# Layer 0 preparation: offset range by ScalarE sums of Relu, and a third depthwise tap on TensorE

## The chip, the cores and the metric

The kernel runs on one core of a Trainium2 chip. The metric is the device time of one execution in microseconds, as the median of several runs; lower is better. A NeuronCore has five engines with instruction queues of their own: TensorE (PE in the profile, with its weight loads as PEld), VectorE (DVE), ScalarE (ACT), GpSimd (POOL) and SyncE (SP). Each works off its queue in order and waits on semaphores for the others. DMA transfers are issued from the queues of SyncE, ScalarE or GpSimd.

## The reference

A four layer network on an input of 8 images of 56 x 56 pixels with 128 channels. Only the first half of layer 0, a deformable convolution, is touched:

```python
xp = x @ w_in + b_in
h = conv3x3_depthwise(x, dw_w) + dw_b
h = (h - bn_m) * bn_g / sqrt(bn_v + 1e-05) + bn_b
h = gelu(h)
offset = (h @ w_off + b_off).reshape(N, H, W, 4, 9, 2)
mask = softmax((h @ w_msk + b_msk).reshape(N, H, W, 4, 9), axis=-1)
y = dcn_core(xp, offset, mask) @ w_out + b_out
...
```

`dcn_core` samples `xp` bilinearly at nine points per pixel and group, each shifted by its own offset, and sums them with the mask. The rest of layer 0 is a norm, an MLP and a second norm. Layer 1 is a whitening transform of the whole tensor, layer 2 attention with a mixture of experts, layer 3 linear attention with another. They are not touched.

## The kernel before

`conv_layer` prepares, for all 8 images, what the sampling needs, and keeps it in device memory: the input transposed (`q.xT`), offsets and mask (`q.om`), and the projection `xp` in overlapping strips with a border of zeros (`q.strips`). Then one number decides on the branch: if no offset is larger than 1 in size, `sample_near` runs, otherwise `sample_any` in a loop over the images. The branch is at L400 and L401. With these inputs `sample_near` is taken, and its first instruction on GpSimd, the memset of `wide` (L467), waits for the last transfer of `om`.

The preparation is one loop over n from -1 to 8 with functions that are called in this order: `hidden` of image n-1, `image` and `first_taps` of image n+1, `other_taps` of image n, after every odd image `projection` of the pair, and `offsets` of image n-1. Images lie in pairs in two tiles `xp0` and `xp1`, with borders of zeros.

- `image` (L257): one load of `xs` by SyncE; 28 transposes on TensorE into PSUM (`p_x`, L266); seven copies to the padded image by ScalarE (L271); seven shifted copies `xT` by ScalarE (L276), each written to device memory by SyncE (L279). `xT` has two buffers.
- `first_taps` (L309): the first `NTE` of the nine taps of the depthwise convolution as matmuls with diagonal matrices (`taps`, made at L223), in seven groups of eight image rows, accumulated in PSUM (`p_dw`, L315) and copied to `acc` by ScalarE (L322). `NTE` is 2.
- `other_taps` (L325): the taps left over, seven per image, on VectorE: `acc = xp * dw + acc` over 128 x 3136 elements (L327).
- `hidden` (L336): seven Gelus on ScalarE with the folded batch norm (L341), to `hT`.
- `offsets` (L350): 28 matmuls (`p_om`, L356), seven adds of the bias on VectorE (L363), the largest and the smallest offset by two reductions on VectorE (L365, L366), the mask's softmax (`mask_softmax`, L424 to L435: maximum, subtraction, Exp on ScalarE at L432, sum, reciprocal, product, the others on VectorE), and the write of `om` by SyncE (L370).
- `projection` (L281): 56 matmuls per pair (`p_in`, L288), 14 adds of the bias on VectorE (L295), and twelve writes to `strips` by SyncE (L301 to L305).

All these share one PSUM pool of eight buffers (tag "m"), so a matmul group starts only when a buffer has been read out. Tiles of the pool `l0h` (`xs`, `xT`, `acc`, `hT`, `om`, `pj`, `msum`) have two buffers. The order of the instructions in each queue is not that of the text: a scheduler interleaves the functions of different images by its own estimate of durations. After the loop, L393 takes the largest entry of `far` per partition, a transpose (L395) and L397 the largest of all, and L398 compares it with 1.

Before the loop GpSimd clears the tile `zero` (L237), and ScalarE's queue issues its transfers into the borders of `strips`: two large ones (L240) and sixteen small ones (L245). Its first copy L271 comes behind these.

Of the kernel before, what the change touches and what calls it, by code (L numbers as in the profile page):

```python
# [8 lines left out]
F32 = mybir.dt.float32  # L9
I32 = mybir.dt.int32  # L10
U32 = mybir.dt.uint32
AF = mybir.ActivationFunctionType
ALU = mybir.AluOpType
AX = mybir.AxisListType
# [3 lines left out]
NB, IH, IW, C = 8, 56, 56, 128  # L18
S = IH * IW
T = 112  # L20
NT = S // T
# [6 lines left out]
GP = GRP * NP  # L28
# [3 lines left out]
VW = IW + 4  # L32
PH, PX, NX = 7, 4, 14
SW = PX + 4
# [1 line left out]
R4 = 4 * C  # L36

NPX = 6
NTE = 2


WB, WCOLS, WSTEP, WITER, WEPS = 64, NB * S * C // 64, 9, 5, 0.01
# [85 lines left out]
def conv_layer(tc, k, x, w, z):  # L128

    nc = tc.nc  # L130
    n_batch = x.shape[0]
    with ExitStack() as ctx:
        cp = ctx.enter_context(tc.tile_pool(name="l0c", bufs=1))
# [62 lines left out]
        gam = row_bc(nc, cp, w["gamma2"], T, "gam2r")  # L196
        nc.vector.tensor_tensor(q.sft2, q.sft2, gam, ALU.mult)

        far = cp.tile([T, 2 * n_batch], F32, name="far")
        near = cp.tile([1, 1], I32, name="near")  # L200
        with ExitStack() as pre:
            ip = pre.enter_context(tc.tile_pool(name="l0i", bufs=1))
# [11 lines left out]
                "b_om",  # L214
            )
            b_om = b_om.unsqueeze(1).to_broadcast([T, GT, 3 * GP])

            dw = ip.tile([C, 9], F32, name="dw")
            nc.sync.dma_start(dw, w["dw_w"].rearrange("c a b d -> c (a b d)"))

            taps = ip.tile([C, NTE, C], F32, name="taps")
            for j in range(NTE):
                nc.vector.tensor_scalar(taps[:, j], k.ident, dw[:, j : j + 1], None, ALU.mult)  # L223
# [9 lines left out]
            nc.vector.tensor_tensor(bn_t, bn_t, bn_s, ALU.mult)  # L233
            nc.vector.tensor_tensor(bn_t, bn_t, bn_b, ALU.add)

            zero = ip.tile([NX * n_batch, 2 * SW * C], F32, name="zero")
            nc.gpsimd.memset(zero, 0.0)  # L237
            rows = q.strips.rearrange("n k y s c -> (n k) y (s c)")
            for y in (0, VW - 2):
                nc.scalar.dma_start(  # L240
                    rows[:, y : y + 2].rearrange("k y s -> k (y s)"), zero
                )
            for n in range(n_batch):
                for at in (q.strips[n, 0, :, :2], q.strips[n, NX - 1, :, SW - 2 :]):
                    nc.scalar.dma_start(  # L245
# [63 lines left out]
            def first_taps(xp):  # L309

                acc = hp.tile([C, IH, IW], F32, name="acc")
                for y in range(0, IH, 2 * GT):
                    p = ps.tile([C, 2 * GT, IW], F32, tag="m", name="p_dw")
                    for j in range(NTE):
                        nc.tensor.matmul(  # L315
# [3 lines left out]
                            start=(j == 0),  # L319
                            stop=(j == NTE - 1),  # L320
                        )
# [3 lines left out]
            def other_taps(xp, acc):  # L325
                for j in range(NTE, 9):
                    nc.vector.scalar_tensor_tensor(  # L327
                        acc,
                        xp[:, j // 3 : j // 3 + IH, j % 3 : j % 3 + IW],
                        dw[:, j : j + 1],  # L330
                        acc,
                        ALU.mult,
                        ALU.add,
                    )
# [15 lines left out]
            def offsets(n, hT):  # L350

                om = hp.tile([T, NT, 3 * GP], F32, name="om")
                for r in range(PH):
                    p = ps.tile([T, GT, 3 * GP], F32, tag="m", name="p_om")
                    for i in range(GT):
                        nc.tensor.matmul(  # L356
                            p[:, i, :],
                            hT[:, r, i].rearrange("p a b -> p (a b)"),
                            w_om,
                            start=True,  # L360
                            stop=True,
                        )
                    nc.vector.tensor_tensor(om[:, r * GT : (r + 1) * GT, :], p, b_om, ALU.add)  # L363
                off = om[:, :, : 2 * GP]
                nc.vector.tensor_reduce(far[:, 2 * n : 2 * n + 1], off, AX.XY, ALU.max)  # L365
                nc.vector.tensor_reduce(  # L366
                    far[:, 2 * n + 1 : 2 * n + 2], off, AX.XY, ALU.min, negate=True
                )
                mask_softmax(nc, hp, om)
                nc.sync.dma_start(q.om[n], om)  # L370


# [4 lines left out]
            for n in range(-1, n_batch + 1):  # L377
                if n > 0:
                    hT = hidden(accs.pop(n - 1))
                if n + 1 < n_batch:  # L380
                    image(n + 1, place(n + 1))
                    accs[n + 1] = first_taps(place(n + 1))
                if 0 <= n < n_batch:
                    other_taps(place(n), accs[n])
                    if n % 2 == 1:
                        for b in range(2):
                            projection(n - 1, pairs[n // 2 % 2], b)
                if n > 0:
                    offsets(n - 1, hT)
# [5 lines left out]
            nc.tensor.transpose(p, top, k.ident[:T, :T])  # L395
            one = ip.tile([1, 1], F32, name="far_one")
            nc.vector.tensor_reduce(one, p, AX.X, ALU.max)  # L397
            nc.vector.tensor_scalar(near, one, 1.0, None, ALU.is_le)  # L398

        taken = nc.values_load(near[0:1, 0:1], min_val=0, max_val=1)  # L400
        with tc.If(taken > 0) as both:  # L401
# [22 lines left out]
def mask_softmax(nc, pool, om):  # L424

    n_t = om.shape[1]
    m = om[:, :, 2 * GP :].rearrange("p t (q g) -> p t g q", g=GRP)
    msum = pool.tile([T, n_t, GRP], F32, name="msum")
    mb = msum.unsqueeze(3).to_broadcast([T, n_t, GRP, NP])
    nc.vector.tensor_reduce(msum, m, AX.X, ALU.max)  # L430
    nc.vector.tensor_tensor(m, m, mb, ALU.subtract)
    nc.scalar.activation(om[:, :, 2 * GP :], om[:, :, 2 * GP :], AF.Exp)  # L432
    nc.vector.tensor_reduce(msum, m, AX.X, ALU.add)
    nc.vector.reciprocal(msum, msum)
    nc.vector.tensor_tensor(m, m, mb, ALU.mult)  # L435
# [1854 lines left out]
@with_exitstack  # L2290
def conv_attn_hybrid_kernel(ctx, tc, a, out):
    cp = ctx.enter_context(tc.tile_pool(name="const", bufs=1))
    dp = ctx.enter_context(tc.tile_pool(name="between", bufs=1, space=DRAM))
    n_b = a["x"].shape[0]
    k = make_consts(tc, cp)
    z = dp.tile([IH, n_b, IW, C], F32, name="z")
    y = dp.tile([IH, n_b, IW, C], F32, name="y")
    w = {n.removeprefix("L0_conv_"): v for n, v in a.items() if n.startswith("L0_")}
    conv_layer(tc, k, a["x"], w, z)
    whiten_layer(tc, k, z, y)  # L2300
    token_layers(tc, k, a, y, out.rearrange("n h w c -> n (h w) c"))
# [42 lines left out]
```

## Time and profile before

| | us |
|---|---|
| median of three runs | 7727.34 |
| the three runs | 7716.75, 7727.34, 7728.98 |
| the profiled execution | 7718.14 |
| its span, first to last instruction | 7716.3 |
| first tap on VectorE (L327) | at 55.0 |
| product of the last softmax ends (L435) | at 434.6 |
| first instruction of the next stage (L467) | at 441.1 |

The profile gives, for one execution, when each instruction of each engine ran and what its engine waited for before it. A group line has the source line, the engine, the operation, output <- inputs with their sizes, the count, the busy time and the mean of one, and after the bar the idle time of the engine just before such instructions with the releasers. The share of an engine over the whole span says little here, since the program has stages with different limits; the preparation is the first 441 us of 7716 and is read by itself. One matmul of 32 bit floats appears as two rows.

### The profile page before, as it was taken

The numbers are of one execution on the slowest core, as the hardware profiler recorded it, in microseconds if no ns is written. First come the engines' busy times: TensorE is split into PE (matmuls) and PEld (weight loads), VectorE is DVE, ScalarE is ACT, GpSimd is POOL, SyncE is SP. The second block draws the span as 40 slices with busy tenths as digits, with TensorE's granted clock in tenths as the row PEclk, the third lists the DMA queues.
The fourth block names the chain that finished last, engine by engine and source line by source line (L and its number), as shares of the span: only waits on it lengthen the run. The fifth ranks groups of instructions, "written<-read, shape, count | busy, mean of one in ns | idle before, by whom it ended". The sixth has DMA issues, their size and how long they took to land. (4 is left out here: it accounts for less than half of the span.)

```text
span 7716.3 us, 157926 instructions
## 1 busy us (share of the span) xinstructions
PE 6482.3 (84%) x59883; PEld 2880.7 (37%) x59883; DVE 5284.8 (68%) x9856; ACT 4142.6 (54%) x6467; POOL 2935.1 (38%) x2555
## 2 busy tenths in 40 slices
PE   6659999556899999999999999999999997556654
PEld 4446666334233323323323323333333333245532
DVE  7975564366677777777777777777777776366752
ACT  4424444122666666666666666666666664056740
POOL 0011111022444444444444444444444443434653
PEclk8768898777999999999999999999999998788766
DMA  5453443376788778778778778778778775543543
GB/s 155 137 119 76 86 95 65 82 240 207 199 203 197 193 192 199 189 192 201 191 184 204 188 183 207 183 191 205 185 190 206 182 190 137 196 117 107 134 135 130
DMA packets 736303, 1287.38 MB, mean 167 GB/s; under 512 B 117698, under 2 KB 503108, under 8 KB 728516
## 3 DMA queue, kind: packets, MB, share of 16 engines
q1 hardware_dynamic: 725556, 1260.76, 65.1%
q0 software_dynamic: 6144, 12.60, 0.6%
q8 instruction: 484, 7.93, 0.5%
q10 hardware_dynamic: 3824, 3.68, 0.2%
q14 instruction: 295, 2.42, 0.1%
HBM read 286.04 MB, written 197.81 MB: 63 GB/s over the span
## 5 line engine op out<-in xcount | busy, mean ns | idle before, releaser
L1260 ACT ACTIVATE e<-p_s 128x768 f32<-128x768 f32 (+2 forms) x3712 | 2887.8, 830 | 1584.9 <-PE p_s L1252 1329.8
L1298 POOL COPY x<-sq 32x1152 f32<-32x1152 f32 x1792 | 2059.2, 1149 | 2067.6 <-PE p_s L1252 1330.0
L1271 DVE STREAM_TRANSPOSE sq<-e 128x768 f32<-128x768 f32 x2688 | 2434.5, 950 | 567.3 <-ACT e L1260 312.9
L1252 PE MATMUL p_s<-q,kT 32*128 32x384 f32 (+2 forms) x14848 | 1888.6, 548 | 33.6 <-ACT e L1260 18.6
L1305 PE MATMUL av<-e,va 128*32 128x384 f32 (+2 forms) x14848 | 1645.3, 515 | 30.4 <-DVE acc L1324 20.7
L1305 PE MATMUL avx<-x,va 128*32 128x384 f32 x10752 | 1138.3, 496 | 69.5 <-issue 40.2
L1252 PEld LDWEIGHTS p_s<-q,kT 32*128 32x128 f32 (+1 forms) x14848 | 654.8, 181 | 1252.6 <-issue 825.4
L1305 PEld LDWEIGHTS av<-e,va 128*32 128x32 f32 (+1 forms) x14848 | 294.5, 108 | 1049.4 <-issue 941.7
L1305 PEld LDWEIGHTS avx<-x,va 128*32 128x32 f32 x10752 | 353.2, 111 | 650.9 <-issue 595.2
L609 POOL TENSOR_TENSOR rs<-rs,mhalf 112x4 f32<-112x4 f32 x112 | 116.1, 1036 | 788.3 <-DVE rs L608 788.3
L1324 DVE TENSOR_TENSOR acc<-acc,avx 128x384 f32<-128x384 f32 x336 | 183.9, 547 | 229.9 <-PE avx L1305 228.6
L121 PE MATMUL p_tr<-ident,xn 112*128 112x112 f32 x672 | 134.6, 341 | 187.4 <-DVE xn L112 141.8
L1141 POOL TENSOR_TENSOR rs<-rs,mhalf 112x4 f32<-112x4 f32 (+2 forms) x136 | 168.1, 1236 | 269.3 <-DVE ntop L1942 123.8
L525 ACT COPY wT<-p_w 88x448 f32<-88x448 f32 x152 | 138.0, 922 | 194.1 <-PE p_w L523 161.4
L1990 ACT ACTIVATE xn<-t,ms,rs 112x128 f32<-112x128 f32 x448 | 185.3, 488 | 76.4 <-DVE ms L1983 76.4
L327 DVE SCALAR_TENSOR_TENSOR acc<-xp,dw,acc 128x3136 f32<-128x3136 f32 x56 | 194.3, 3478 | 31.3 <-ACT acc L322 31.2
L637 PE MATMUL p_f<-x1T,w 128*128 128x448 f32 x448 | 205.6, 583 | 4.4 <-DVE x1T L632 2.7
L121 PEld LDWEIGHTS p_tr<-ident,xn 112*128 112x128 f32 x672 | 98.7, 169 | 285.0 <-issue 185.1
L1385 POOL TENSOR_TENSOR rs<-rs,mhalf 128x3 f32<-128x3 f32 (+1 forms) x72 | 58.5, 815 | 365.0 <-DVE rs L1384 343.0
L523 PE MATMUL p_w<-ident,wide 112*88 112x112 f32 x896 | 146.5, 303 | 58.6 <-DMA px<-strips 34.1
L621 DVE TENSOR_TENSOR y<-y,p_rs 128x448 f32<-128x448 f32 x112 | 69.3, 619 | 176.6 <-PE p_rs L614 176.6
L122 ACT COPY xT<-p_tr 128x448 f32<-128x448 f32 x112 | 59.6, 532 | 229.8 <-PE p_tr L121 203.7
(354 smaller groups left out, 7830.9 us busy)
## 6 DMA issues: line engine op xcount, KB each, us to landing
x<-sq SPq DMA_DIRECT2D x5376, 144.0 KB
w<-in_L_ffn_weight_dram SPq DMA_DIRECT2D x64, 1024.0 KB
px<-strips SPq DMA_DIRECT2D x64, 616.0 KB
va_d<-va SPq DMA_DIRECT2D x16, 1600.0 KB
xT_d<-xT SPq DMA_DIRECT2D x112, 224.0 KB
xT<-xT_d SPq DMA_DIRECT2D x112, 224.0 KB
kT_d<-kT SPq DMA_DIRECT2D x16, 1568.0 KB
t<-t_a SPq DMA_DIRECT2D x16, 1568.0 KB
```

Of the source, the lines that this page charges most:

```text
L121: nc.tensor.transpose(p[:, i, :], src[:, i, :], k.ident[:T, :T])
L327: nc.vector.scalar_tensor_tensor(acc, xp[:, j // 3 : j // 3 + IH, j % 3 : j % 3 + IW], dw[:, j : j + 1], acc, ALU.mult, ALU.add,)
L523: nc.tensor.transpose(p[:, g], around[:, :, g], k.ident[:T, :T])
L637: nc.tensor.matmul(p, q.w1[:, f * 128 : (f + 1) * 128], x1T, start=True, stop=True)
L1141: nc.gpsimd.tensor_tensor(rs, rs, k.mhalf[:m, :n], ALU.pow)
L1252: nc.tensor.matmul(ss[j // 2][:m, j % 2, :width], kT[rows, 128 * i : 128 * i + m], q[rows, :width], start=True, stop=True,)
L1260: nc.scalar.activation(e[:m, 2 * j : 2 * j + 2, :width], ss[j][:m, :, :width], AF.Exp)
L1271: nc.vector.transpose(sq[:, :, i, j : j + 2].rearrange("p s j c -> p j s c"), exps[u, b, a, i][:, j : j + 2, :QB].rearrange("p j (s c) -> ...
L1298: nc.gpsimd.tensor_copy(*moves.pop(0))
L1305: nc.tensor.matmul(out, keys[u, b][1][:m, i, j, :], e[j], start=start, stop=stop)
L1324: nc.vector.tensor_tensor(to, to, in_order(av), ALU.add)
L1990: nc.scalar.activation(out[:, i], x[:, i], AF.Identity, bias=ms[:, i : i + 1], scale=rs[:, i : i + 1])
```

## The change

The range of the offsets is no longer taken by a maximum and a minimum on VectorE. Four ScalarE activations per image compute Relu(offset - 1) and Relu(-offset - 1), each over half of the image's positions, and their accumulator output gives the sum of each per partition. `far` therefore has four columns per image, and the final test asks whether the largest sum is at most 0 instead of whether the largest size is at most 1. The four come behind the softmax in the text, they read the offsets only. A tile `over` takes their elementwise results, a constant column `minus` their bias.

`NTE` goes from 2 to 3: a third diagonal matrix is made, `first_taps` issues three matmuls per group instead of two, and `other_taps` has six taps per image instead of seven. The tile `zero` is half as long, and the rows of zeros at the top and the bottom of the strips are written by four transfers instead of two.

```diff
--- before.py
+++ after.py
@@ -36,7 +36,7 @@
 R4 = 4 * C
 
 NPX = 6
-NTE = 2
+NTE = 3
 
 
 WB, WCOLS, WSTEP, WITER, WEPS = 64, NB * S * C // 64, 9, 5, 0.01
@@ -196,7 +196,7 @@
         gam = row_bc(nc, cp, w["gamma2"], T, "gam2r")
         nc.vector.tensor_tensor(q.sft2, q.sft2, gam, ALU.mult)
 
-        far = cp.tile([T, 2 * n_batch], F32, name="far")
+        far = cp.tile([T, 4 * n_batch], F32, name="far")
         near = cp.tile([1, 1], I32, name="near")
         with ExitStack() as pre:
             ip = pre.enter_context(tc.tile_pool(name="l0i", bufs=1))
@@ -214,6 +214,8 @@
                 "b_om",
             )
             b_om = b_om.unsqueeze(1).to_broadcast([T, GT, 3 * GP])
+            minus = ip.tile([T, 1], F32, name="minus")
+            nc.vector.memset(minus, -1.0)
 
             dw = ip.tile([C, 9], F32, name="dw")
             nc.sync.dma_start(dw, w["dw_w"].rearrange("c a b d -> c (a b d)"))
@@ -233,13 +235,11 @@
             nc.vector.tensor_tensor(bn_t, bn_t, bn_s, ALU.mult)
             nc.vector.tensor_tensor(bn_t, bn_t, bn_b, ALU.add)
 
-            zero = ip.tile([NX * n_batch, 2 * SW * C], F32, name="zero")
+            zero = ip.tile([NX * n_batch, SW * C], F32, name="zero")
             nc.gpsimd.memset(zero, 0.0)
             rows = q.strips.rearrange("n k y s c -> (n k) y (s c)")
-            for y in (0, VW - 2):
-                nc.scalar.dma_start(
-                    rows[:, y : y + 2].rearrange("k y s -> k (y s)"), zero
-                )
+            for y in (0, 1, VW - 2, VW - 1):
+                nc.scalar.dma_start(rows[:, y], zero)
             for n in range(n_batch):
                 for at in (q.strips[n, 0, :, :2], q.strips[n, NX - 1, :, SW - 2 :]):
                     nc.scalar.dma_start(
@@ -362,11 +362,18 @@
                         )
                     nc.vector.tensor_tensor(om[:, r * GT : (r + 1) * GT, :], p, b_om, ALU.add)
                 off = om[:, :, : 2 * GP]
-                nc.vector.tensor_reduce(far[:, 2 * n : 2 * n + 1], off, AX.XY, ALU.max)
-                nc.vector.tensor_reduce(
-                    far[:, 2 * n + 1 : 2 * n + 2], off, AX.XY, ALU.min, negate=True
-                )
                 mask_softmax(nc, hp, om)
+
+                over = ip.tile([T, NT // 2, 2 * GP], F32, name="over")
+                for a in range(4):
+                    nc.scalar.activation(
+                        over,
+                        off[:, a // 2 * NT // 2 : (a // 2 + 1) * NT // 2],
+                        AF.Relu,
+                        bias=minus,
+                        scale=1.0 - 2.0 * (a % 2),
+                        accum_out=far[:, 4 * n + a : 4 * n + a + 1],
+                    )
                 nc.sync.dma_start(q.om[n], om)
 
 
@@ -395,7 +402,7 @@
             nc.tensor.transpose(p, top, k.ident[:T, :T])
             one = ip.tile([1, 1], F32, name="far_one")
             nc.vector.tensor_reduce(one, p, AX.X, ALU.max)
-            nc.vector.tensor_scalar(near, one, 1.0, None, ALU.is_le)
+            nc.vector.tensor_scalar(near, one, 0.0, None, ALU.is_le)
 
         taken = nc.values_load(near[0:1, 0:1], min_val=0, max_val=1)
         with tc.If(taken > 0) as both:
```

## The prediction

> **What bounds the kernel now.** I read the page first. Its chain of waits names only the last output DMA ("DMA 1%"), so it says nothing about a stage in the first 6% of the span. The table by stretches of time does; its columns are busy us of each engine (instructions), granted TensorE clock, DMA share and GB/s. I cut it where VectorE finishes the projection of a pair of images (122.4, 214.7, 306.9, 398.9).
>
> ```profile
> span 7716.3 us, 157926 instructions
> PE 6482.3 (84%) x59883; PEld 2880.7 (37%) x59883; DVE 5284.8 (68%) x9856; ACT 4142.6 (54%) x6467; POOL 2935.1 (38%) x2555
> ...
> 55.00:122.40 67.40, 50.87 (x228) 39.16 (x226) 57.20 (x28) 42.96 (x60) 0.00 (x0) 0.85 0.50 141
> 122.40:214.70 92.30, 67.80 (x339) 51.67 (x338) 89.26 (x57) 47.66 (x62) 0.00 (x0) 0.82 0.56 154
> 214.70:306.90 92.20, 67.91 (x339) 51.75 (x338) 89.17 (x57) 47.40 (x62) 0.00 (x0) 0.81 0.52 150
> 306.90:398.90 92.00, 48.67 (x283) 42.39 (x282) 88.96 (x57) 35.13 (x42) 0.00 (x0) 0.74 0.39 115
> 398.90:445.00 46.10, 10.53 (x105) 10.08 (x103) 33.56 (x31) 2.08 (x2) 3.91 (x1) 0.64 0.65 185
> ```
>
> The preparation is bound by VectorE: 89 of 92 us in each pair, with TensorE at 68 or less and ScalarE at 47. Nothing after it starts before it ends. The groups of the first 520 us (busy, mean ns, idle time before and its releaser) give the prices:
>
> ```profile
> L327 DVE SCALAR_TENSOR_TENSOR acc<-xp,dw,acc 128x3136 f32<-128x3136 f32 x56 | 194.3, 3478 | 31.3 <-ACT acc L322 31.2
> L315 PE MATMUL p_dw<-xp,taps 128*128 128x448 f32 x224 | 98.3, 596 | 14.9 <-DVE om L363 9.0 <-ACT xp L271 6.0
> L365 DVE TENSOR_REDUCE far<-om 112x1 f32<-112x2016 f32 x8 | 18.0, 2255 | 0.0
> L366 DVE TENSOR_REDUCE far<-om 112x1 f32<-112x2016 f32 x8 | 18.0, 2246 | 0.0
> L432 ACT ACTIVATE om<-om 112x1008 f32<-112x1008 f32 x8 | 8.4, 1044 | 39.6 <-DVE om L431 39.6
> ```
>
> The timeline (start, length, instruction, idle time before) shows the slack and where it ends:
>
> ```profile
> 55.00 14.05 DVE L327 SCALAR_TENSOR_TENSOR acc<-xp,dw,acc 128x3136 f32<-128x3136 f32 x4 [29.80 <-ACT acc L322]
> 129.60 10.73 PE L315 MATMUL p_dw<-xp,taps 128*128 128x448 f32 x28
> 154.81 3.36 PE L315 MATMUL p_dw<-xp,taps 128*128 128x448 f32 x4 [0.62 <-ACT xp L271]
> 201.31 2.06 PE L288 MATMUL p_in<-w_in,xp 128*113 128x128 f32 x8 [13.61 <-DVE pj L295]
> 164.58 6.73 ACT L341 ACTIVATE hT<-acc,bn_t,bn_s 128x448 f32<-128x448 f32 x7 [8.52 <-DVE acc L327]
> 441.09 8.78 POOL L467 MEMSET wide<- 112x10416 f32 x1 [417.22 <-DMA om_d<-om]
> ```
>
> VectorE's first tap waits for image 0's copies off TensorE. Later TensorE and ScalarE wait for VectorE, TensorE 13.6 us per pair for PSUM buffers that the bias add of L295 frees. The last line: the next stage opens 6.4 us after the last softmax step (434.64), when the last transfer of om has landed.
>
> **What the skill says.** "ScalarE: Activation LUTs", section "Table sets: the hidden batching unit": Relu is in every table set, so the new Relus load no table. The trace has 14 loads by L341 and L432, and the built order of the changed program also has 14. The section "What ACT_TABLE_LOAD costs" prices an ACTIVATE with a pointer bias at 280 ns + 0.833 ns per element: 1120 ns for 1008. The trace's Exp of the same size, with an immediate bias, takes 1044. "TensorE: Matmul & The Clock Gate", section "Part 1: The HAM clock gate", says that the array falls to half clock after an idle window of some 3.4 us. The trace agrees: four p_dw rows take 3.36 us at 154.81, after a stretch of short bursts, and 28 rows take 10.73 (0.38 each) when warm.
>
> **The change part by part.** In the order of instructions the two programs differ only up to the branch after this preparation, so the rest should only move forward.
>
> *Removed.* A tap starts 3.39 us after the one before it (127.65 to 131.04), a reduction 2.16. VectorE loses 8 x 3.39 = 27.1 and 16 x 2.16 = 34.6: 61.7 us. Its pair goes from 89.0 (14 taps 47.5, reductions 8.6, softmax 2 x 8.4, 14 adds of om 7.4, 14 of pj 8.7) to 73.4.
>
> *Added to TensorE.* A matmul shows as two rows: 14 rows per image x 0.377 = 5.3 us, 42 in all. Its pair without waits was 5.5 (p_x) + 21.2 (p_dw) + 22.7 (p_in) + 11.1 (p_om) = 60.5 and becomes 71.1. That is nearly VectorE's 73.4, so TensorE's waits now count.
>
> *Added to ScalarE.* 32 Relus. No row has this form. Between the Exp's 1.04 and the reduction's 2.25 I take 1.2: the page's 1.12, less some overlap, plus 0.19 for reading the sum (the ACTIVATION_READ_ACCUMULATOR after L1949). Four make 4.9 us per image. The built order puts Relus among the Gelus of the next image and, for odd images, ahead of the copies L271 of the image after. A Relu waits for its half of om; queued behind it are those copies, and TensorE's p_dw waits for them.
>
> *Zero writes.* Four issues of half the size instead of two on ScalarE's queue: about +1.4 us at 0.68 each, covered because that queue then waits 7.0 us for bn_v. The memset before them is shorter, 0.9 for 1.8. The third diagonal is one more 0.24 us operation before 25. I cost all this at nothing; if the cover failed, it would be 1.5 us. The sum test itself stays one compare.
>
> Now the queues, by sums.
>
> 1. *Start to the end of the first projection.* TensorE becomes the chain: p_dw(0) from 40.9, seven cold rows at 0.75, then 35 at 0.377, to 59.3; p_x 2.7; p_dw(1) 15.9; p_x 2.7; p_dw(2) 15.9, to 96.8; p_in 22.7; last add 0.8: 120.3 against 122.3. VectorE starts 5 us later and TensorE fills the 10.97 + 4.58 us that it idled here: **-2**.
> 2. *Pair 2,3* (images). VectorE until the taps of image 2 end: 7 adds 3.9, 6 taps 20.3, softmax less its last step 6.5: 30.7. Then ScalarE: 7 Gelus 6.7, 4 Relus of image 1 4.9, two copies of image 4 0.9: 12.5. Then p_dw(4) 15.9, p_in 22.7, an add 0.8: 82.6. In the old order these copies stood before the Gelus. TensorE thus idles some 7 us and starts cold: seven rows at 0.75 add 2.6. 85.2 against 92.3: **-7**.
> 3. *Pair 4,5.* The same chain, with one tap already done and the adds paced by TensorE: 27.5 + 12.5 + 15.9 + 22.7 + 0.8 + 2.6 = 82.0 against 92.2: **-10**.
> 4. *Pair 6,7.* No more images come in, so VectorE alone: 40.7 + 16.8 + adds 5.5 + 3.7 + pj 10.4 (TensorE fills the last six of 14 at 1.62) = 77.1 against 92.0: **-15**.
> 5. *Tail.* 35.7 us from 398.9 to 434.6 loses four reductions, 8.6; far_top now waits for ScalarE, and Exp stands behind Relus: I give back 1. **-8**.
>
> Sum -42. The profiled execution had 7718.1 (span 7716.3 plus 1.8 around it), giving 7676. The three runs are 7716.8, 7727.3 and 7729.0; with the profiled one the four lie at two levels 11 us apart. I take the middle, 7722.8 less 42: **7680**.
>
> Bounds: a Relu at 1.04 gives back 1 us over the two pairs that have it on their path, at 2.25 it costs 8; cold rows cost 0 to 5 per pair; late copies can vanish (-7 per pair, VectorE then bounds at 77) or be joined by DMA waits of up to 5 per pair. The gain is thus 25 to 58.
>
> **The rivals.**
>
> *A: VectorE still sets all of it.* For: 73.4 is above 71.1, and ScalarE is half idle. The whole 61.7 is saved but for the late start, 5: -57, 7666. Against: the order of the copies above. 15%.
>
> *B: DMA order holds ScalarE.* SyncE issues in order and its queue mixes writes of xT (ScalarE waits for them two deep: 23.2 us before) with writes of strips that wait for VectorE. At 10 more per pair in two pairs: -22, 7701. Against: before, the DMA share is only 0.5 to 0.56. 13%.
>
> *C: slower.* If the xT writes stand behind all 12 strip writes of a pair, ScalarE stalls for their issue time, some 24 us at 2 each (111 to 134), with copies and Gelus behind it, in three pairs: 72 - 42 = +30, 7753. It decides from 14 us per pair on. Against: in the built order mostly one to three strip writes stand between two of xT. With it belongs that the sums are not exactly zero and the branch goes to the general sampler, which no trace here prices. Against that: Relu of a negative value is zero, and zeros add to zero. 7% together.
>
> *D: nothing to see,* the gain eaten by waits of 14 us per pair: 7%.
>
> **The numbers.** My forecast has 58%, A 15, B 13, C 7, D 7. A measurement can tell 0.2%, some 15 us, from no change. A, B and the forecast are all faster by more: 86%; within 7%, slower 7%. The range 7657 to 7706 holds the forecast's bounds around both levels of the runs, most of A and of B.
>
> **What would show it.** Right: VectorE's busy time near 310 instead of 373 up to the branch; pairs of about 85, 82 and 77 us; TensorE idle before p_dw of images 4 and 6, ended by L271; about 38 us of Relus; the memset of wide at about 399. Wrong: a pair with VectorE over 95% busy (A), long waits of L276 for xT_d (B, C), other lines after the branch than before, or p_dw rows slower than 0.38 when warm.

## The result, and the profile after

The changed kernel takes 7677.42 us (median of four runs, 7666.61 to 7685.90) where the kernel before takes 7725.65 us (four runs beside them, 7716.75 to 7728.98). The ratio is 0.9939, with a 95% interval of 0.9921 to 0.9956: 48 us less by the medians. In the profiled executions the span goes from 7716.3 to 7676.2 us, 40 us less.

The preparation can be read more finely than the whole. These are the ends of its parts, each the end of the last bias add of a projection (L295) or of the last softmax product (L442 now, L435 before), and their lengths:

| part | before: end, length | after: end, length | predicted length |
|---|---|---|---|
| start to the first projection | 122.3 | 120.5 | 120.3 |
| pair 2,3 | 214.6, 92.3 | 204.1, 83.6 | 85.2 |
| pair 4,5 | 306.8, 92.2 | 282.8, 78.7 | 82.0 |
| pair 6,7 | 398.8, 92.0 | 360.7, 77.9 | 77.1 |
| tail, to the last softmax product | 434.6, 35.8 | 387.7, 27.0 | some 28 |
| landing of the last `om`, memset of `wide` | 441.1, 6.4 | 397.4, 9.7 | 6.4 |

The table by stretches of time of the changed kernel, cut at its own ends of pairs (columns: start:end, length, then busy us and instructions of PE, PEld, DVE, ACT and POOL, granted TensorE clock, DMA share, GB/s). The first and the last stretch are left out; the sum has them, from 0 to 401.3 us:

```profile
...
55.00:120.50 65.50, 65.50 (x276) 47.15 (x275) 50.90 (x26) 44.77 (x63) 0.00 (x0) 1.00 0.51 144
120.50:204.10 83.60, 75.12 (x367) 57.86 (x367) 77.06 (x52) 53.40 (x76) 0.00 (x0) 0.92 0.63 169
204.10:282.80 78.70, 73.55 (x366) 55.64 (x365) 70.74 (x49) 51.64 (x74) 0.00 (x0) 0.98 0.58 160
282.80:360.70 77.90, 53.58 (x297) 44.89 (x297) 73.91 (x51) 48.18 (x63) 0.00 (x0) 0.80 0.55 156
...
sum 401.30, PE 297.48 PEld 227.64 DVE 312.44 ACT 221.82 POOL 16.72; mean PE 49.58 PEld 37.94 DVE 52.07 ACT 36.97 POOL 2.79
```

The table shows three different limits. In the first stretch TensorE is busy for all of 65.50 us, where it was idle for 16.5 before. In the two pairs in the middle no engine is full: VectorE 77.06 of 83.6 and 70.74 of 78.7, TensorE 75.12 and 73.55. In pair 6,7 VectorE is the fullest again, with 73.91 of 77.9. VectorE's sum up to the branch is 312.4 us (before 373.4).

The groups of the first 520 us, now:

```profile
L327 DVE SCALAR_TENSOR_TENSOR acc<-xp,dw,acc 128x3136 f32<-128x3136 f32 x48 | 167.2, 3485 | 36.7 <-ACT acc L322 36.4
L315 PE MATMUL p_dw<-xp,taps 128*128 128x448 f32 x336 | 134.7, 561 | 14.9 <-ACT xp L271 14.9
L369 ACT ACTIVATE over<-om,minus 112x1008 f32<-112x1008 f32 x32 | 36.1, 1127 | 29.0 <-DVE om L363 28.8
```

TensorE's wait before `p_dw` is now for the copies L271 alone, 14.9 us. Before, the sum was the same, but 9.0 us of it were waits for VectorE's adds.

What the copies wait for in turn is seen in the timeline of the changed kernel (start, length, instruction, idle time before and its releaser), at the middle of pair 2,3:

```profile
147.69 3.40 DVE L327 SCALAR_TENSOR_TENSOR acc<-xp,dw,acc 128x3136 f32<-128x3136 f32 x1
151.12 3.96 ACT L341 ACTIVATE hT<-acc,bn_t,bn_s 128x448 f32<-128x448 f32 x4 [5.45 <-DVE acc L327]
155.07 1.14 ACT L369 ACTIVATE over<-om,minus 112x1008 f32<-112x1008 f32 x1
156.11 0.19 ACT L369 ACTIVATION_READ_ACCUMULATOR over<-om,minus 112x1 f32 x1
156.20 1.17 ACT L341 ACTIVATE hT<-acc,bn_t,bn_s 128x448 f32<-128x448 f32 x1
157.17 1.09 ACT L369 ACTIVATE over<-om,minus 112x1008 f32<-112x1008 f32 x1
...
161.24 1.11 ACT L369 ACTIVATE over<-om,minus 112x1008 f32<-112x1008 f32 x1
162.24 0.21 ACT L369 ACTIVATION_READ_ACCUMULATOR over<-om,minus 112x1 f32 x1
162.33 3.11 ACT L271 COPY xp<-p_x 128x448 f32<-128x448 f32 x7
162.91 17.91 PE L315 MATMUL p_dw<-xp,taps 128*128 128x448 f32 x42 [4.63 <-ACT xp L271]
```

VectorE's last tap of image 2 ends at 151.1. Then ScalarE works without a gap, seven Gelus and four Relus in turn, and only then comes the first copy of image 4, which releases TensorE at 162.91. This chain was written down ahead; it is there with the same members, but for one copy where two were counted.

The end of the stage, same view (SPq is SyncE's queue of transfers):

```profile
374.68 1.99 SPq L305 DMA_DIRECT2D strips<-pj  x1
380.01 8.10 SPq L377 DMA_DIRECT2D om_d<-om  x2
385.77 1.94 DVE L442 TENSOR_TENSOR om<-om,msum 112x1008 f32<-112x1008 f32 x1
397.40 8.78 POOL L474 MEMSET wide<- 112x10416 f32 x1 [374.30 <-DMA om_d<-om]
```

The last product ends at 387.7 and the second of the two writes of `om`, image 7's, is issued then (image 6's at 380.0). The memset of `wide`, which waits for its landing, comes 9.7 us later, not 6.4. This part was not foreseen, and takes back some 3 us.

### The profile page after: what moved, and what is told of

It reads as the page before. It is cut to its first block, busy times and chain, and to the rows that moved or that the text cites. A ratio compares the mean times of both kernels' runs of the same rounds, so it can differ in the third digit from the quotient of the medians.

```text
span 7676.2 us, 158198 instructions
## 1 busy us (share of the span) xinstructions
PE 6527.3 (85%) x59995; PEld 2901.6 (38%) x59995; DVE 5222.9 (68%) x9834; ACT 4177.5 (54%) x6531; POOL 2935.1 (38%) x2555
## 5 line engine op out<-in xcount | busy, mean ns | idle before, releaser
L1312 PE MATMUL avx<-x,va 128*32 128x384 f32 x10752 | 1145.1, 496 | 60.3 <-issue 37.0
L532 ACT COPY wT<-p_w 88x448 f32<-88x448 f32 x152 | 138.0, 922 | 196.2 <-PE p_w L530 196.1
L327 DVE SCALAR_TENSOR_TENSOR acc<-xp,dw,acc 128x3136 f32<-128x3136 f32 x48 | 167.2, 3485 | 36.7 <-ACT acc L322 36.4
## 6 DMA issues: line engine op xcount, KB each, us to landing
xT_d<-xT SPq DMA_DIRECT2D x112, 224.0 KB
xT<-xT_d SPq DMA_DIRECT2D x112, 224.0 KB
```

Source lines behind the costliest of these rows:

```text
L327: nc.vector.scalar_tensor_tensor(acc, xp[:, j // 3 : j // 3 + IH, j % 3 : j % 3 + IW], dw[:, j : j + 1], acc, ALU.mult, ALU.add,)
L1312: nc.tensor.matmul(out, keys[u, b][1][:m, i, j, :], e[j], start=start, stop=stop)
```

## The experiments

Each kernel below has one profiled execution; times are compared only where a kernel was executed four or five times. The marks are those of the table above: the last product, and the memset of `wide`, where the next stage opens. Behind the memset the kernels do the same work, but single executions differ there by up to 21 us (7275 to 7297 us from the memset to the end). The changed kernel's own nine executions lie between 7665.4 and 7687.8 us. So the memset, not the time of one execution, is the gauge for an edit to the preparation: single executions with the copies ahead and with the small zeros by GpSimd took 7685.0 and 7690.2 us, though both reach the memset some 5.5 us earlier than the changed kernel.

| run | ends of the projections | last product | memset of `wide` |
|---|---|---|---|
| before | 122.3, 214.6, 306.8, 398.8 | 434.6 | 441.1 |
| changed | 120.5, 204.1, 282.8, 360.7 | 387.7 | 397.4 |
| third tap alone | 119.1, 204.0, 289.4, 374.7 | 410.3 | 416.6 |
| Relus alone | 124.1, 208.4, 292.0, 375.6 | 401.7 | 416.0 |
| copies ahead of the Relus | 121.3, 197.7, 275.9, 352.6 | 379.7 | 391.9 |
| small zeros by GpSimd | 112.8, 196.2, 275.0, 352.8 | 379.8 | 391.8 |
| four taps | 145.4, 224.0, 305.0, 374.0 | 400.1 | 417.4 |
| last projection early | 120.7, 204.0, 282.5, 340.5 | 385.4 | 391.7 |
| all three moves | 111.5, 188.9, 267.1, 323.9 | 370.5 | 376.8 |

### The two halves of the change, each alone

The third tap alone is the kernel before with `NTE = 3` and the zero writes of the changed one; the reductions stay on VectorE:

```diff
-NTE = 2
+NTE = 3
```

> Three taps on TensorE, the range still by two VectorE reductions per image. My theory (each part removes VectorE time, but TensorE sets the first 120 us): first projection done at about 120.5 as with the whole change, then three pairs at VectorE's 82.0 plus 3 of waits, 85 each, the tail at the old 35.7; the memset of wide at 418 to 421 against 441.1 before. Rival (the parts simply add, each worth its VectorE time): 27.1 less 5 of later start, 419. The two differ only when this run is added to the one with the Relus alone: additive parts give the 43.7 us of the whole change, my theory gives about 55.

The Relus alone are the changed kernel with two taps on TensorE:

```diff
-NTE = 3
+NTE = 2
```

> The range by ScalarE Relus, two taps on TensorE as before. My theory: first projection done at 122.3 as before, then three pairs at VectorE's 80.4 plus 3 of waits, 83.5 each, the tail some 8 shorter than before; the memset of wide at 406 to 410 against 441.1. So this part alone should bring 31 to 35 of the 43.7, and the two parts alone together 50 to 58, more than both at once, since TensorE and the copies of ScalarE take over once both are in. Rival (additive): about 21 here, memset at 420, so that the sum is 43.7.

Measured: the memset of `wide` at 416.6 with the tap alone and at 416.0 with the Relus alone, gains of 24.5 and 25.1 us. The table by stretches of time, first of the tap alone, then of the Relus alone:

```profile
55.00:119.10 64.10, 64.10 (x272) 46.51 (x271) 50.88 (x26) 43.30 (x61) 0.00 (x0) 1.00 0.51 147
119.10:204.00 84.90, 74.09 (x367) 56.53 (x366) 81.99 (x55) 46.94 (x62) 0.00 (x0) 0.92 0.62 167
204.00:289.40 85.40, 73.97 (x366) 56.42 (x365) 82.14 (x55) 47.80 (x62) 0.00 (x0) 0.92 0.59 165
289.40:374.70 85.30, 53.15 (x297) 44.88 (x297) 81.98 (x55) 35.33 (x42) 0.00 (x0) 0.80 0.43 124
```

```profile
55.00:124.10 69.10, 51.91 (x236) 39.96 (x235) 57.20 (x28) 43.80 (x62) 0.00 (x0) 0.85 0.51 142
124.10:208.40 84.30, 66.02 (x339) 51.62 (x338) 80.79 (x52) 52.57 (x76) 0.00 (x0) 0.84 0.58 157
208.40:292.00 83.60, 66.28 (x338) 51.90 (x337) 80.65 (x52) 58.30 (x82) 0.00 (x0) 0.84 0.60 172
292.00:375.60 83.60, 48.70 (x283) 42.42 (x283) 80.52 (x53) 42.97 (x58) 0.00 (x0) 0.76 0.45 132
```

With either half alone VectorE stays within 2.9 to 3.5 us of full in every pair, so each half gives nearly all that it takes off VectorE. Together they don't add up: at the last product the two gains are 24.3 and 32.9, in sum 57.2, and the change has 46.9. Of the 10.3 us that are missing, 6.7 are missing in pair 2,3, 1.9 in pair 4,5, and 1.1 each in pair 6,7 and in the tail, less 0.4 won at the start. So most of the loss lies where, in the changed kernel, TensorE waits for ScalarE's copies and VectorE is no longer full; the next experiment tests these copies.

The tap alone came 1.4 us ahead of its expectation; the Relus alone missed theirs by 6 us and more. Their stage itself was as fast as foreseen (last product at 401.7), but the landing of the last `om` took 14.3 us instead of 6.4. For that reason the test that was written down, the sum of the two gains at the memset, doesn't decide: it is 49.6, between the 43.7 of additive parts and the 55 of the theory. With what the changed kernel shows at the same place, this opened a second question: what holds the last landing?

### Whether the copies hold TensorE

```diff
             for n in range(-1, n_batch + 1):
+                if n + 1 < n_batch:
+                    image(n + 1, place(n + 1))
                 if n > 0:
                     hT = hidden(accs.pop(n - 1))
                 if n + 1 < n_batch:
-                    image(n + 1, place(n + 1))
                     accs[n + 1] = first_taps(place(n + 1))
```

> The changed kernel with image called ahead of hidden in the loop, so that the copies L271 of an even image stand ahead of most Gelus and Relus in ScalarE's queue. If these copies hold TensorE in pairs 2,3 and 4,5 (my step 2 and 3), p_dw of image 4 starts at about 158 instead of 162.9 and warm, p_dw of image 6 likewise 4 to 6 us earlier, and the memset of wide comes at 384 to 388 instead of 397.4. If VectorE sets the pairs (rival A), the order of the copies does not matter: 396 to 398.

Measured: `p_dw` of image 4 begins at 157.8 instead of 162.9, and pair 2,3 takes 76.4 us instead of 83.6, pair 4,5 78.2 instead of 78.7, pair 6,7 76.7 instead of 77.9. In the table by stretches of time of this kernel VectorE is the fullest engine in the first and the last of the three pairs, and level with TensorE in the middle one:

```profile
121.30:197.70 76.40, 72.57 (x367) 56.24 (x366) 73.48 (x50) 52.53 (x76) 0.00 (x0) 0.98 0.64 173
197.70:275.90 78.20, 73.80 (x367) 57.47 (x366) 73.74 (x50) 53.51 (x78) 0.00 (x0) 0.96 0.62 171
275.90:352.60 76.70, 53.01 (x297) 44.73 (x295) 73.43 (x50) 46.88 (x63) 0.00 (x0) 0.82 0.56 160
```

In TensorE's timeline of this kernel, before image 4 and before image 6:

```profile
154.28 3.72 PE L266 MATMUL p_x<-ident,xs 112*128 112x112 f32 x24 [3.83 <-DVE om L363]
157.79 16.61 PE L315 MATMUL p_dw<-xp,taps 128*128 128x448 f32 x42
231.22 4.74 PE L266 MATMUL p_x<-ident,xs 112*128 112x112 f32 x24 [4.40 <-DVE om L363]
```

The last product comes 8.0 us earlier than in the changed kernel. The wait for the copies is real in pair 2,3: 7.2 us come back there, all that the two halves miss in it. Pair 4,5 gains only 0.5 us. There `p_dw` of image 6 begins 38.1 us after the start of the pair, with the copies late it was 37.9: TensorE now waits 4.4 us for PSUM buffers, which VectorE's adds free, before it can transpose image 6. The memset, expected at 384 to 388, comes at 391.9. It gains only 5.5 of the 8.0, since the landing takes 12.2 us.

`p_dw` of image 4 takes 16.6 us here, 17.9 in the changed kernel and 16.0 where all its rows are fast. The granted clock tells why. In the changed kernel it falls to half at 153.0, after TensorE has stood still for 3.3 us for PSUM buffers, and returns at 166.7, 3.8 us into `p_dw`. Here it falls at 155.7, after a wait of 3.8 us for the same buffers, and returns at 159.1, 1.3 us into `p_dw`. The group loses about half of the time at half clock, 1.9 and 0.6 us. This is the clock gate that the prediction took from the Trainium skill, "TensorE: Matmul & The Clock Gate", section "Part 1: The HAM clock gate".

### Whether TensorE is close behind

```diff
-NTE = 3
+NTE = 4
```

> A fourth tap on TensorE: 14 more rows of 0.377 us per image, 5.3 us; VectorE loses another 3.39 us per image. If TensorE with ScalarE's copies is the chain, as my steps 1 to 3 have it, each p_dw that stands on it costs 5.3 us more: three of them before the first projection ends (120.5 to about 136), one in each of the next two pairs (83.6 and 78.7 to about 87 and 84, less what the later start of VectorE gives back), the last pair 77.9 less up to 6.8. The memset of wide then comes at 411 to 418 instead of 397.4. If VectorE were still the engine that sets all (rival A), it loses 27 us in all and the memset comes before 380.

Measured: memset at 417.4, 20 us later than with three taps, although VectorE has less to do. The table by stretches of time of this kernel (the first cut, at 223.0, is 1 us ahead of the end of pair 2,3):

```profile
145.40:223.00 77.60, 77.60 (x360) 56.73 (x360) 63.62 (x46) 55.74 (x78) 0.00 (x0) 1.00 0.66 179
223.00:305.00 82.00, 82.00 (x403) 61.13 (x403) 68.42 (x50) 55.44 (x78) 0.00 (x0) 1.00 0.58 165
305.00:374.00 69.00, 58.23 (x311) 47.23 (x310) 63.45 (x48) 42.76 (x57) 0.00 (x0) 0.90 0.52 153
```

TensorE is busy in every us of the pairs in the middle, so the rival is out. The fourth tap moves work from VectorE, which has room, to the engine that has none. The first projection ends at 145.4, later than the 136 expected: `p_dw` of image 2 also waits 3.2 us for its copies and takes 24.2 us where a warm one takes 21.2, and the last bias add stands behind a tap. The pairs in the middle (78.7 and 81.0) come out shorter than the 87 and 84 expected, the last at 69.0. The last product is 12.4 us later than with three taps; the other 7.6 us at the memset are the landing, which takes 17.3.

### What holds the start

The sixteen small writes of zeros (L245) are issued by GpSimd's queue instead of ScalarE's:

```diff
-                    nc.scalar.dma_start(
+                    nc.gpsimd.dma_start(
```

> The changed kernel with the sixteen small writes of zeros (L245) issued from GpSimd's queue instead of ScalarE's. ScalarE's first copies then need not wait for 18.8 us of issues until 40.75. If TensorE's chain from its first p_dw sets the first projection, p_dw of image 0 starts at about 36.5 (end of p_x) instead of 41.3 and everything after it moves by the same 5: first projection done at 115.5, memset of wide at 392. If the load of the first image or the borders' memset is what comes last, nothing moves.

Measured: `p_dw` of image 0 begins at 35.7 instead of 41.3 and is warm (16.1 us for 19.0), and the first projection ends at 112.8, not at the 115.5 expected. The timeline of the changed kernel shows what was in the way (ACTq is ScalarE's queue of transfers); below it, that of this kernel:

```profile
21.85 18.80 ACTq L245 DMA_DIRECT2D strips<-zero  x16
40.75 3.15 ACT L271 COPY xp<-p_x 128x448 f32<-128x448 f32 x7 [20.23 <-DMA strips<-zero]
41.33 18.95 PE L315 MATMUL p_dw<-xp,taps 128*128 128x448 f32 x42 [4.90 <-ACT xp L271]
```

```profile
31.49 0.53 ACT L271 COPY xp<-p_x 128x448 f32<-128x448 f32 x1 [11.05 <-PE p_x L266]
35.67 16.07 PE L315 MATMUL p_dw<-xp,taps 128*128 128x448 f32 x42
```

In the changed kernel ScalarE's first copy stands behind the issue of these sixteen transfers until 40.7. Without them it waits for the first transposes, at 31.5, and TensorE goes from the transposes to `p_dw` without a pause. The last product gains 7.9 us where 5 were expected, since the rows are also fast from the start. The memset gains 5.6 and comes at 391.8 for the expected 392, but by luck: the landing takes 12.0 us and gives the rest back.

### What holds the last landing

Theory: the twelve strip writes of the last projection, issued by the same SyncE queue, are still being moved when the last `om` is written, and a shorter tail leaves them less time. In the first test these writes are left out for images 6 and 7, with zeros written there ahead of the loop:

```diff
                     left, right = max(k0, 1), min(k0 + ks, NX - 1)
+                    if n == n_batch - 2:
+                        continue
...
+            for y in range(2, VW - 2):
+                nc.gpsimd.dma_start(rows[(n_batch - 2) * NX :, y], zero[(n_batch - 2) * NX :])
```

> Leaves out the twelve strip writes of the projection of images 6 and 7 (some 6 MB); zeros go there before the loop, by GpSimd's queue. Theory: in the changed kernel the last transfer of om lands 9.7 us after the last softmax product, and not 6.4, because these writes are still being drained. Without them the landing comes 5 to 6.5 us after the product (about 394 for the memset of wide, less or more what the early zeros do to the start). Rival: the last om write of 1.3 MB takes that long by itself, or something else holds its issue: the landing stays at 9 to 10 us after the product.

In the second nothing is left out, and the last projection is called ahead of the taps of image 7 instead of behind them:

```diff
                 if 0 <= n < n_batch:
+                    if n == n_batch - 1:
+                        for b in range(2):
+                            projection(n - 1, pairs[n // 2 % 2], b)
                     other_taps(place(n), accs[n])
-                    if n % 2 == 1:
+                    if n % 2 == 1 and n < n_batch - 1:
```

> The projection of images 6 and 7 is called ahead of the taps of image 7, so its twelve strip writes start some 20 to 30 us earlier, with nothing left out and the work of each engine the same. If the drain of these writes is what delays the last om, the landing comes 6 to 7 us after the last softmax product instead of 9.7, and with the product at its place (388) the memset of wide comes at 394 to 395. If the order of VectorE's queue gets worse by it, the product itself comes later than 388. Rival (the last om write takes that long by itself): 9 to 10 us after the product, memset at 397 or later.

Measured: without the writes the landing takes 6.6 us, with the last product 27.1 us behind the last bias add, as in the changed kernel (27.0). (The memset itself is late, 414.5: beside the early zeros ScalarE waits 26.6 us for the writes of `xT` instead of 10.2, and the first projection ends some 18 us late.) With the last projection early the landing takes 6.3 us and the memset comes at 391.7, 5.7 us earlier than in the changed kernel. That is more than expected (394 to 395), because the last product also came 2.4 us earlier.

The stretches of time of the changed kernel from its last bias add to the last strip write, to the last product, and to the landing; then the 11 us before the last product of the kernel without the writes; then the kernel with the early projection, from its last bias add to the last strip write and to the last product:

```profile
360.70:376.70 16.00, 10.27 (x105) 10.09 (x103) 14.81 (x19) 10.75 (x16) 0.00 (x0) 0.94 0.82 217
376.70:387.70 11.00, 0.34 (x1) 0.08 (x1) 10.31 (x9) 2.45 (x5) 0.00 (x0) 0.50 0.80 213
387.70:397.40 9.70, 0.00 (x0) 0.00 (x0) 0.01 (x1) 0.00 (x0) 0.00 (x0) 0.50 0.52 181
```

```profile
396.80:407.80 11.00, 0.34 (x1) 0.08 (x1) 10.31 (x9) 2.43 (x5) 0.00 (x0) 0.50 0.36 123
```

```profile
340.50:369.30 28.80, 8.78 (x71) 8.43 (x69) 27.84 (x19) 15.07 (x18) 0.00 (x0) 0.70 0.81 227
369.30:385.40 16.10, 4.56 (x25) 4.13 (x25) 14.50 (x14) 10.05 (x14) 0.00 (x0) 0.66 0.57 162
```

In the changed kernel the DMA engines are at 80% and 213 GB/s on average in the 11 us before the last `om` is issued: there is a backlog. Part of what they move is image 6's `om` (1.3 MB), issued 7.8 us before image 7's. That this write alone holds the landing is a rival, and the kernel without the strip writes excludes it: it has the same two writes 7.8 us apart, a share of 36% ahead of the second, and lands in 6.6 us. With the early projection the share is 57% on average, 15% from 381 to 383 and 6% from 383 to 385, just before the last issue.

The backlog doesn't slow the last write as a whole. In the second profile of the changed kernel, which lands in 12.2 us, the DMA share, a mean over 16 DMA engines, is about 1 from 389.4 to 392.4, has fallen to 0.14 in the us before 395.4, and is 0.06, with 24 GB/s, in each us from 396.4 to 399.4. One of 16 engines alone would show 0.06, so the landing seems to wait for a single engine that came late to its part of `om`. The stretch at 0.06 is there too with the copies ahead, with the Relus alone and with four taps (2 to 4 us each), and for 2 us in the first profile of the changed kernel.

All kernels with these writes follow one rule. The table sets the time between the end of the last strip write's issue and the end of the last product against the landing:

| run | strip write to product, us | landing, us |
|---|---|---|
| tap alone | 19.4 | 6.3 |
| before | 18.9 | 6.4 |
| all three moves, two runs | 17.6, 17.7 | 6.3, 6.3 |
| last projection early | 16.1 | 6.3 |
| copies ahead | 11.1 | 12.2 |
| changed, two runs | 11.0, 11.0 | 9.7, 12.2 |
| small zeros by GpSimd | 11.0 | 12.0 |
| copies ahead and small zeros | 10.8 | 12.1 |
| Relus alone | 8.9 | 14.3 |
| four taps | 6.8 | 17.3 |

Where the product comes 16 us or more after the last strip write, the landing takes 6.3 to 6.4 us, whatever else the kernel does. Where it comes after 11 us or less, the two add up to 21 to 24 us: the backlog sets the end then, and not the softmax. Between 11 and 16 us nothing was measured.

### A version with all three moves

The edits of the copies, the small zeros and the last projection together:

> Three moves together, nothing left out: image n+1 is called ahead of hidden of image n-1 (copies before Relus), the sixteen small zero writes go to GpSimd's queue, and the last projection is called ahead of the taps of image 7. The first took 8.0 us off the last product, the second 7.9, the third should only take the landing from 12 to about 6.5 us. If they add up: product at 372, memset of wide at 379 to 382, time 15 to 18 us under the changed kernel (about 7660, ratio to before 0.9915). If the first and second move the same wait, or the transfers need their 36 to 42 us after the last projection whatever is done, the memset stays at 388 or later and the time at 7668 or more.

Measured: last product at 370.5, landing 6.3, memset at 376.8, 20.6 us ahead of the changed kernel. At the last product the three moves bring 17.2 us together and 18.3 alone in sum, so there they nearly add up; the rest at the memset is the shorter landing. The median time is 7668.25 us (four runs), the ratio to the kernel before 0.9922 (0.9905 to 0.9938). That is 9 us less than the changed kernel's median, not 20. A comparison on one chip was to tell whether the rest is given back:

> The changed kernel as it is, beside the next two on one chip. Nothing differs from the run on record: memset of wide at 397, last landing 9.7 us after the last softmax product, ratio to the kernel before 0.994. The stretches behind the branch may differ by up to 20 us from execution to execution, since they did so between kernels that are the same there.

> The copies ahead of the Relus and the small zero writes on GpSimd's queue, without moving the last projection. If the two waits are separate (8.0 and 7.9 us off the last product each), the product ends at 371 to 373; the last strip writes then end 7 to 9 us before the om write is issued, and by the drain theory its landing takes 10 to 13 us: memset at 382 to 385. With the landing at 6.4 us whatever is queued ahead of it, it would be 378.

> The three moves together once more, for a comparison on the same chip with the changed kernel: memset of wide at 377, 20 us before it. If nothing behind the branch depends on when the branch is reached, its time is 20 us lower, some 0.26%, and its ratio to the kernel before about 0.991; if part is given back behind the branch, as the first median of it (9 us lower) would have it, the ratio is 0.9925 or more.

With two of the moves the product ends at 370.5 and the landing takes 12.1 us, as the backlog has it. The changed kernel's second profile has a landing of 12.2 us, not 9.7, and so its memset 3 us later. The times:

| beside 7717.09 us before | median us | ratio, 95% interval | memset of `wide` |
|---|---|---|---|
| the changed kernel | 7678.27 | 0.9939 (0.9924 to 0.9953) | 400.4 |
| copies ahead and small zeros | 7665.95 | 0.9926 (0.9911 to 0.9941) | 382.5 |
| all three moves | 7668.27 | 0.9928 (0.9913 to 0.9942) | 377.9 |

Both versions have medians 10 to 12 us below the changed kernel's, but the intervals overlap, and the early projection's 4.6 us at the memset can't be seen in the time. The memsets promised 18 and 22 us. For the kernel with all three moves a ratio of 0.991 was to mean that nothing is given back behind the memset, and 0.9925 or more that part is. The measured 0.9928 points to the second, but its interval begins at 0.9913.

Behind the memset the kernels with all three moves took 7294.7 and 7288.6 us, the one with two moves 7286.2, the changed kernel 7278.8 and 7285.5, the kernel before 7275.2. Whether that is chance or something behind the branch gives time back when it is reached earlier was not settled. The stretches that differ are the attention of layer 2 (4546 and 4552 us with all three moves, 4538 in both profiles of the changed kernel, but 4536 with two moves) and one in the last layer (151 and 141 with all three moves, 141 in the other three profiles), and no run isolates them. For chance speaks that the time behind the memset doesn't follow the memset in the other kernels: those that reach it at 414 to 417 took from 7278.0 us (tap alone) to 7295.9 (without the last strips). That either version beats the changed kernel is likely, not shown.

## Why the prediction was right

The forecast, 7680 us by a gain of 42, stands against 7677.4 and a gain of 46.9 at the last softmax product, 43.7 at the memset, 40 in the profiled span. That the memset is so near is partly luck. Up to the last product the kernel gained 4.9 us more than forecast, and the landing, which the forecast left as it was, took 3.2 us of that back in this profile and 5.7 in the second, whose gain at the memset is 40.7.

*The first projection* came at 120.5 for 120.3. (The terms of that step add up to 120.0, since 59.3 leads to 96.5, not 96.8.) TensorE is the chain, as said: `p_dw` of image 0 from 41.3 to 60.3, with cold rows (the first seven take 5.6 us, 0.80 each, where warm ones take 0.38), and `p_dw` of the other two images at 16.0 us each.

*Pair 2,3.* The chain's first part, VectorE to the end of the taps of image 2, was put at 30.7 us and took 30.6 (120.5 to 151.1). ScalarE's part was put at 12.5 with two copies and took 11.8 with one: the first group of `p_dw` needs rows that the first copy brings, since the three taps on TensorE lie in one kernel row. The cold rows cost 1.9 us (17.9 less 16.0), not 2.6. Together 1.6 us less than predicted. TensorE's wait for the copies was 4.6 us, not some 7, and it isn't what brought the clock down here: that was the wait for PSUM buffers ahead of the transposes, as the test of the copies shows. The prediction's sign for the idle window, the four rows of 3.36 us at 154.81 in the kernel before, shows half speed, but the pauses just ahead of it were of 0.62 us each; it is the changed kernel that shows a wait of over 3 us ahead of the half clock.

*Pair 4,5.* VectorE's part took 27.3 for 27.5. ScalarE's took 10.5 for 12.5: one copy instead of two, and only three of the four Relus ahead of it, as the timeline shows:

```profile
240.28 1.09 ACT L369 ACTIVATE over<-om,minus 112x1008 f32<-112x1008 f32 x1
241.28 0.18 ACT L369 ACTIVATION_READ_ACCUMULATOR over<-om,minus 112x1 f32 x1
241.37 0.51 ACT L271 COPY xp<-p_x 128x448 f32<-128x448 f32 x1
241.78 1.13 ACT L369 ACTIVATE over<-om,minus 112x1008 f32<-112x1008 f32 x1
241.93 17.65 PE L315 MATMUL p_dw<-xp,taps 128*128 128x448 f32 x42 [4.13 <-ACT xp L271]
```

With 1.7 us of cold rows for 2.6 the pair is 3.3 us shorter than predicted. Here TensorE's wait for the copies, 4.1 us, did bring the clock down, at 241.8. The order of work held and these terms were too large. But this pair hardly needed the copies: called earlier, they brought 0.5 us, and the wait for PSUM buffers, which the step left out, took their place.

*Pair 6,7* took 77.9 for 77.1, with VectorE as the fullest engine, 73.9 us busy. (By the prediction's own terms, 89.0 less two taps and four reductions, VectorE's pair is 73.6, not 73.4.)

*The tail* lost 8.8 us for the 8 predicted. What the step left out is the landing behind it: it was taken as 6.4 us as before, and 9.7 in one profile and 12.2 in another were measured. The tail is shorter than the backlog of the strip writes allows. That these writes are the cause is shown by the kernel without them, and the early projection agrees.

*The prices.* A Relu was put at 1.2 us; where nothing stands between them, one starts 1.26 us after the other (363.78, 365.04, 366.30 in the timeline). The Trainium skill, "ScalarE: Activation LUTs", section "What ACT_TABLE_LOAD costs", led to an estimate of 1120 ns for the activation; the trace has 1136 as the median of 32, and 0.19 us more for reading the sum. The new Relus brought no table load: this trace too has 14 by L341 and the Exp. The zero writes were costed at nothing, with a bound of 1.5 us. They held ScalarE's queue for 6.96 us instead of 1.36:

```profile
11.94 6.96 ACTq L242 DMA_DIRECT2D strips<-zero  x4
```

The cover held all the same: before, the activation behind them (L229) waited 7.0 us for `bn_v` and ran at 22.4, now (L231) it runs at 20.2 without a wait. The first copy came 0.4 us later (40.75 for 40.33), because the sixteen small writes took 18.8 us instead of 17.7.

*The rivals.* A, VectorE sets all of it, is excluded by its share in the pairs in the middle (92% and 90%), by what the copies alone bring in pair 2,3, and by the fourth tap. B and C, a queue of SyncE that holds ScalarE, are excluded by ScalarE's waits for writes of `xT`: 10.2 us in the whole preparation, against 23.2 before. C's other case, the general sampler, did not come: the memset of `wide` belongs to `sample_near`. D needed waits of 14 us per pair; the pairs are shorter than forecast or within 0.8 us of it.

## What to carry to other kernels

When work is taken from the fullest engine, sum the other engines to the same mark before adding up the gains: here two halves gave 24 and 33 us alone and 47 together, since a chain through TensorE and ScalarE became the limit, in pair 2,3 above all, when VectorE had lost both. An activation that is put on an idle engine still stands in front of something, so look at which copy is next in that queue and call that first. Then look again, since the next wait can be close behind: in pair 4,5 it was the PSUM buffers. And where a stage ends with the landing of a transfer, a shorter tail can only be worth as much as the backlog of earlier transfers lets through; start the big writes earlier rather than the last one faster. Here that was worth 5.7 us at the memset, too little to be seen in the time of the whole.

## What the runs showed of the hardware

The issue of a strip write takes longer right behind others: the first two of a projection take 0.35 and 0.43 us, the following ones 1.8 to 2.7 us each. A backlog of the DMA engines alone doesn't do that: image 6's `om`, 3.3 us behind the last strip write, is issued in 0.34 us, with the engines at 75% in the 2 us before and 91% in the 2 us after. After the last strip write's issue the DMA engines work on at 80% for 11 us, and the rest of the strip writes and the two writes of `om` together need 21 to 24 us from then on. Where this backlog holds the landing, its final 2 to 4 us run at a DMA share of 0.06 and 24 GB/s.

Four writes of zeros took 6.96 us of ScalarE's queue where two writes of the same bytes in all took 1.36. Each of the four issues is short (0.31 to 0.43 us), but the third starts 4.6 and the fourth 6.7 us after the first; what holds them back the profile doesn't show. And the landing of the last `om` differs between executions of the same kernel when it is held by the backlog (9.7 and 12.2 us), but is 6.3 to 6.6 us in all kernels where it isn't.
